# Image copies and Square of layer 2's norm at steps 8 and 12 of the run loop instead of step 15

## The chip, the cores and the metric

The kernel runs on one core of one Trainium2 chip. The core has five engines that work side by side, each through its own queue in order: TensorE (PE, matmuls; PEld is its weight load), VectorE (DVE), ScalarE (ACT), GpSimd (POOL) and SyncE (SP, which here only issues DMAs). Sixteen DMA engines move data between HBM and the on-chip memories. Matmuls write to PSUM. The metric is device time in microseconds (us); less is better.

## The reference, cut to what matters

Four layers follow each other on an image of shape (2, 64, 96, 96): attention over all pixels, a Mamba layer over the pixels in one sequence, a Mamba layer over rows and columns in both directions, and a 3 x 3 filter made from the image's mean. The change is in the third, which the kernel calls layer 2. Its core, with x as (b, c, t, f):

```python
def _rmsnorm(x, w):
    return x * rsqrt(mean(x * x, axis=-1) + EPS) * w

def _mamba(u, p):
    x, z = split(u @ in_proj_w.T)
    x = silu(causal_conv4(x) + conv_b)
    dt, B, C = split(x @ x_proj_w.T)
    dt = softplus(dt @ dt_proj_w.T + dt_proj_b)
    # for each of 128 channels and 16 states, along the sequence:
    h = exp(dt * A) * h + dt * B * x
    y = sum over states of h * C
    return ((y + x * Dp) * silu(z)) @ out_proj_w.T

def _bimamba(u, pf, pb):      # forward, and backward on the flipped sequence
    yf = _mamba(_rmsnorm(u), pf) + u
    yb = flip(_mamba(_rmsnorm(flip(u)), pb) + flip(u))
    return concat(yf, yb)

xt = sequences along t;  xt = xt + _bimamba(xt, P[0], P[1]) @ tlin_w + tlin_b
xf = sequences along f;  xf = xf + _bimamba(xf, P[2], P[3]) @ flin_w + flin_b
```

The norm weight is folded into the projection in the kernel, and both directions share one normalised input.

## The kernel before, in words

**Units.** Layers 1 and 2 are one stream of 120 units, run by `Mamba.run`. A unit is 768 positions (`CH`) of one direction of one batch. Layer 1 gives 24 units. Layer 2 gives 96: first 48 along t, in 24 pairs of a forward and a backward unit over the same eight sequences, then 48 along f. The image is kept on the chip in `k.xb`. Along t a unit reads it with a stride of 96 elements, along f without. The two units of a pair share one `norm`, which belongs to the first (`norm.unit is u`).

**Steps.** A unit has 128 channels x 16 states, that is 16 scans (`STEPS`) of 128 partitions x 768. The loop `for n in range(begin, ...)` in `run` does one step of one unit in each turn:

- `read` (SP, five steps ahead): two DMAs fetch the rows that the step needs from `rows` in HBM into `spread`, one of six buffers.
- `decay` (ScalarE, three steps ahead, L853): two exponentials into h, one of nine buffers.
- `inputs` (VectorE, L863, two steps at a time): `place` in PSUM is `spread` times B.
- `scan` (VectorE, L878), and right behind it on POOL h times C (L879).
- `shared` (TensorE, L857): B for half a unit, into the one PSUM tile for it, issued at step 6 for the second half and at step 14 for the next unit's first half.
- `gather` (TensorE, L888, two steps later): sums h over the states into y.

**Pieces.** All else that a unit needs is cut into pieces, and the table `PIECES` gives each an offset in steps from the unit's own step 0. A piece with offset -49 runs 49 turns before, at step -49 mod 16 = 15 of an earlier unit. Within a turn, `decay` comes first, then `inputs`, `scan` and `gather`, then the pieces of that step whose names are in `reads`, then the others, in the order of the table. The order of instructions on each engine is the order in which this loop issues them; it is written by hand (`manual_schedule`), with no planner. The pieces that matter here, all on one pair's clock (E: the first unit of a pair, O: the second; the norm of a pair is made two pairs ahead, while another pair's units are being scanned):

| piece | engine, line | step |
|---|---|---|
| `gate_read` | ScalarE L772 | 9 of each unit |
| `tail_0`, `tail_1` (the pair before's result) | TensorE L671 | E9, E10 |
| `y_half`, `silu` | ScalarE L892, L775 with two table loads | 10 |
| `tail_read` | ScalarE L924 | E11 |
| `step_mm`, `step_read` | TensorE L671, ScalarE L792, L793 | 11, 13 |
| `step_exp` | ScalarE L797 to L799 | 14 |
| `step_kept` | POOL L806, waits for L799 | 15 |
| `norm_square` | ScalarE L714 twice, L715 | E15 |
| `step_log` | ScalarE L803 | 15 |
| `c_mm`, `c_read` | TensorE, ScalarE L832 | 15, 1 of the next unit |
| `norm_mean` | TensorE L693, into the PSUM tile that `c_read` frees | O1 |
| `norm_root`, `norm_scale` | ScalarE L723, L724, POOL L737 | O3, O10 |
| `step_sum`, `step_dt`, `step_u` | POOL L809, L812, L816, and a memset L820 | 1, 5, 7 |
| `step_write` | SP L825: two DMAs of the unit's dt and dt x to `rows` | 8 |
| `conv`, `conv_read` | TensorE L761, ScalarE L766 | 5, 7 |

The dt that is written at step 8 is that of the next unit; its first `read` follows at step 11 on the same queue, behind the write and behind the reads for steps 14 and 15 of the running unit.

**Buffers.** The normalised input xn has two buffers, sq one. Pieces that need a PSUM tile for a product share one tile `m`, so each waits until the reader of the one before is done.

Of the kernel before, what the change touches and what calls it, by code (L numbers as in the profile page):

```python
# [20 lines left out]
AF = mybir.ActivationFunctionType  # L21
# [10 lines left out]
D_STATE, DT_RANK, D_CONV = 16, 4, 4  # L32
HALF = 4 * W
CH = 2 * HALF
# [33 lines left out]
def rows_of(b):  # L68
    return slice(b * C, (b + 1) * C)
# [551 lines left out]
class Mamba:  # L621
# [79 lines left out]
            u.p = self.mm([(self.t.centre[rows_of(u.b)], self.halves(u.image))])  # L701

    def norm_square(self, u):
        if u.norm.unit is not u:
            return
        u.norm.x = self.work("xn", D_CONV - 1 + CH)
        u.sq = self.work("sq", bufs=1)
        x = u.norm.x[:, D_CONV - 1 :]
        if u.carry:
            self.nc.scalar.activation(u.sq, u.p, AF.Square)  # L710
            self.nc.scalar.copy(x, u.p)
        else:
            for j in range(2):
                self.nc.scalar.copy(x[rows_of(j)].rearrange("p (n t) -> p n t", n=u.image.shape[1]), u.image)  # L714
            self.nc.scalar.activation(u.sq, x, AF.Square)  # L715

    def norm_mean(self, u):
        if u.norm.unit is u:
# [197 lines left out]
    def tail_read(self, u):  # L916
# [10 lines left out]


    PIECES = (
        (-51, "norm_centre"),  # L930
        (-49, "norm_square"),
        (-47, "norm_mean"),
# [34 lines left out]
    def run(self, units, first, n_first, other):  # L967
# [8 lines left out]
        table = [[] for _ in range(self.STEPS)]  # L976
        for offset, name in self.PIECES:
            table[offset % self.STEPS].append((name not in reads, offset, name))
        begin, end = self.PIECES[0][0], self.PIECES[-1][0]


        self.nc.scalar.preload_act_table_set("natural_log_exp_and_others")
        first(0)
        for offset, name in self.PIECES:
            if offset < 0:
# [326 lines left out]
```

## Time and profile before

| | us |
|---|---|
| three runs | 7981.94, 7980.62, 7986.1 |
| median | 7981.94 |
| profiled span | 7974.9 |

The profile is of one execution. Its page gives the busy time of each engine, the chain of work that ended last, and the costliest groups of instructions as: line, engine, operation, what is written <- what is read, shapes, count, then busy us and mean ns of one, then the idle time of the engine just before these instructions and what ended it. "L879 POOL" is line 879 of the kernel on POOL. A list of waits has: engine and line that waited, what it waited for, us in total, times, longest us. A timeline has: start, duration, engine, line, what it does, and in brackets the idle time before and what ended it; neighbours of one kind are merged (x2, x4).

Layer 0 takes the first 2.65 ms or so, layer 1 goes on to about 3.82 ms, layer 2 to 7.89 ms. In layer 2, between 3390 and 7900 us, VectorE is busy 4308 us of 4510, POOL 4063, TensorE 3807 and ScalarE 3405, and the DMA engines are busy for 87 to 90%.

### The profile page before, as it was taken

How to read it: one execution, taken by the hardware profiler on the slowest of the kernel's cores; microseconds unless marked ns; L12 is line 12 of the kernel's file. 1: busy time of each engine (PE TensorE's matmuls, PEld its weight loads, DVE VectorE, ACT ScalarE, POOL GpSimd, SP SyncE). 2: the span in 40 equal slices, each digit the busy share in tenths (PEclk: the TensorE clock that was granted, in tenths of full speed). 3: DMA queues.
4: the chain of work that ended last, by engine and by line, in shares of the span. 5: the costliest groups of instructions: out<-in, count | busy, mean ns of one | idle time of the engine just before them, and what ended most of it. 6: DMA issues, size and time to landing. Idle time of an engine off the chain costs nothing.

```text
span 7974.9 us, 82275 instructions
## 1 busy us (share of the span) xinstructions
PE 7063.0 (89%) x24578; PEld 3122.4 (39%) x24578; DVE 6749.1 (85%) x5524; ACT 5214.3 (65%) x6953; POOL 4724.4 (59%) x3146
## 2 busy tenths in 40 slices
PE   9999999999999788888888888888888888888887
PEld 3333333333333344444444444444444444444443
DVE  6666666666666599999999999999999999999999
ACT  4444444444444577777777777777777777777773
POOL 0000000000000399999888889989889999999985
PEclk9999999999999899999999999999999999999999
DMA  1000000000000388888888888988998899898985
GB/s 43 1 1 1 1 1 1 3 5 5 5 5 3 144 303 317 312 304 325 312 332 325 328 329 329 342 334 328 334 337 334 340 341 347 336 336 335 343 335 205
DMA packets 593806, 1726.06 MB, mean 216 GB/s; under 512 B 65988, under 2 KB 67140, under 8 KB 592840
## 3 DMA queue, kind: packets, MB, share of 16 engines
q1 hardware_dynamic: 591904, 1717.68, 57.9%
q8 instruction: 196, 3.21, 0.2%
q10 hardware_dynamic: 1448, 3.05, 0.1%
q14 instruction: 258, 2.11, 0.1%
HBM read 1522.68 MB, written 197.79 MB: 216 GB/s over the span
## 4 chain that ended last, share of the span: by engine, by line
PE 11%; DMA 10%; ACT 9%; issue 8%; POOL 8%; DVE 4%; SPq 1%; DVEq 0%; ACTq 0%; POOLq 0%
DMA spread<-rows 7%; PE y L888 6%; POOL h L879 6%; ACT h L853 3%; DMA rows<-dtu 3%; PE mm L671 2%; DVE place L863 2%; DVE h L878 1%; PE conv L761 1%; POOL dtu L812 1%; POOL dtu L816 1%; PE y L885 1%; DVE xa L1211 1%; ACT xn L714 1%; PE mm L693 1%
## 5 line engine op out<-in xcount | busy, mean ns | idle before, releaser
L879 POOL TENSOR_TENSOR h<-h,C 128x768 f32<-128x768 f32 x1920 | 3452.4, 1817 | 347.4 <-DVE h L878 310.3
L888 PE MATMUL y<-h,pair 128*128 128x384 f32 x7680 | 2809.6, 510 | 103.4 <-POOL h L879 102.7
L878 DVE TENSOR_TENSOR_SCAN h<-h,place 128x768 f32<-128x768 f32 x1536 | 2606.3, 1737 | 13.6 <-ACT h L853 13.0
L888 PEld LDWEIGHTS y<-h,pair 128*128 128x128 f32 x7680 | 1513.6, 200 | 1306.8 <-POOL h L879 239.6
L311 ACT ACTIVATE e<-f_exp 128x1536 f32<-128x1536 f32 x864 | 1206.4, 1448 | 1224.4 <-PE f_exp L301 1224.4
L853 ACT ACTIVATE h<-spread,xa 128x384 f32<-128x384 f32 x3072 | 1734.3, 608 | 367.0 <-DMA spread<-rows 343.6
L367 DVE TENSOR_TENSOR acc_e<-acc_e,e 128x1536 f32<-128x1536 f32 x792 | 1389.9, 1755 | 683.7 <-ACT e L311 644.8
L863 DVE TENSOR_TENSOR place<-spread,B 128x768 f32<-128x768 f32 x1920 | 1735.0, 948 | 261.9 <-PE B L857 250.8
L340 POOL TENSOR_TENSOR xa<-xa,t_att 64x512 f32<-64x512 f32 x36 | 45.3, 1259 | 2612.3 <-ACT t_att L338 2612.3
L318 PE MATMUL y_att<-e,xb 128*64 128x512 f32 x5184 | 1243.7, 601 | 0.0
L301 PE MATMUL f_exp<-theta,phi 64*128 64x512 f32 x5184 | 1234.6, 607 | 1.0 <-DVE xb L284 0.5
L301 PEld LDWEIGHTS f_exp<-theta,phi 64*128 64x128 f32 x5184 | 466.4, 186 | 754.5 <-issue 460.6
L874 DVE TENSOR_TENSOR_SCAN h<-h,state,place 128x384 f32<-128x384 f32 x768 | 714.0, 990 | 0.0
L318 PEld LDWEIGHTS y_att<-e,xb 128*64 128x64 f32 x5184 | 341.6, 136 | 830.5 <-issue 829.2
L853 ACT ACTIVATE h<-spread,rates 128x384 f32<-128x384 f32 x768 | 433.0, 608 | 150.3 <-DMA spread<-rows 137.5
L885 PE MATMUL y<-raw,xa 128*128 128x384 f32 x384 | 220.4, 663 | 210.5 <-ACT yg L895 182.8
L671 PE MATMUL mm<-raw,xa 128*128 128x384 f32 x768 | 301.2, 517 | 99.2 <-ACT xb L924 91.5
L766 ACT ACTIVATE raw<-conv,cols 128x768 f32<-128x768 f32 x120 | 108.2, 902 | 305.2 <-PE conv L761 240.9
L806 POOL TENSOR_TENSOR kept<-dtu,kept 128x768 f32<-128x768 f32 x120 | 218.3, 1819 | 118.4 <-ACT kept L799 117.9
L761 PE MATMUL conv<-xn,xa 64*128 64x384 f32 (+3 forms) x1536 | 273.1, 494 | 11.7 <-DVE xa L1093 4.0
L892 ACT COPY yg<-y 128x384 f32<-128x384 f32 x120 | 57.4, 478 | 289.7 <-PE mm L671 205.1
L857 PE MATMUL B<-raw,xa 128*128 128x384 f32 x384 | 170.7, 526 | 83.8 <-DVE place L863 83.7
(206 smaller groups left out, 5434.3 us busy)
## 6 DMA issues: line engine op xcount, KB each, us to landing
spread<-rows SPq DMA_DIRECT2D x3840, 384.0 KB, 6.4
rows<-dtu SPq DMA_DIRECT2D x240, 768.0 KB, 5.9
image<-pre SPq DMA_DIRECT2D x11, 384.0 KB, 2.3
xb<-image SPq DMA_DIRECT2D x11, 384.0 KB, 5.8
xa<-in_x SPq DMA_DIRECT2D x1, 2304.0 KB, 23.1
out<-xa ACTq DMA_DIRECT2D x7, 240.0 KB, 2.0
out<-xa SPq DMA_DIRECT2D x1, 1200.0 KB
xa<-in_x SPq DMA_DIRECT2D x3, 384.0 KB, 11.6
```

The lines of the kernel that those rows point to most:

```text
L301: nc.tensor.matmul(fs[j // 3][:, bass.ts(j % 3, NB)], lhsT=phi[at, bass.ts(m // 2, P)], rhs=theta[at, bass.ts(i, NB)], start=True, stop=True,)
L311: nc.scalar.activation(e, f, AF.Exp)
L318: nc.tensor.matmul(y[rows_of(m % 2)], lhsT=g[:, m, :], rhs=es[j // 3][:, bass.ts(j % 3, NB)], start=m < 2, stop=m >= KEYS - 2,)
L367: nc.vector.tensor_add(acc, acc, e)
L671: self.nc.tensor.matmul(o, lhsT=lhsT, rhs=x, start=n == 0, stop=n == len(terms) - 1)
L761: self.nc.tensor.matmul(p3[:, :, o], lhsT=lhsT, rhs=x3[:, :, i], **flags)
L853: self.nc.scalar.activation(h[:, bass.ts(q, HALF)], dt, AF.Exp, scale=u.w.rates[:, n : n + 1])
L863: self.nc.vector.tensor_mul(bx, x, self.B.unsqueeze(1).to_broadcast([P, 2, HALF]))
L874: nc.vector.tensor_tensor_scan(h[:, at], h[:, at], bx[:, at], state[:, q : q + 1], ALU.mult, ALU.add)
L878: nc.vector.tensor_tensor_scan(h[:, way], h[:, way], bx[:, way], 0.0, ALU.mult, ALU.add)
L879: nc.gpsimd.tensor_mul(h2, h2, u.C[:, bass.ts(half, HALF)].unsqueeze(1).to_broadcast([P, 2, HALF]))
L888: self.nc.tensor.matmul(self.y, lhsT=self.t.gather[n], rhs=rhs, start=False, stop=stop)
```

## The change

The piece `norm_square` keeps only what layer 1's units need (`u.carry` is set for these). For layer 2, what it did at E15 in one go is split in two new pieces: `image_0` copies the image to the first 64 partitions of xn at step 8 of E (offset -56), `image_1` copies it to the other 64 and takes the Square at step 12 of E (offset -52). Neither name is in `reads`, so both stand among the last pieces of their step. The convolution and all other pieces stay at their steps. `begin` is the first offset of the table and goes from -51 to -56; the added turns issue nothing.

```diff
     def norm_square(self, u):
-        if u.norm.unit is not u:
-            return
-        u.norm.x = self.work("xn", D_CONV - 1 + CH)
-        u.sq = self.work("sq", bufs=1)
-        x = u.norm.x[:, D_CONV - 1 :]
         if u.carry:
+            u.norm.x = self.work("xn", D_CONV - 1 + CH)
+            u.sq = self.work("sq", bufs=1)
             self.nc.scalar.activation(u.sq, u.p, AF.Square)
-            self.nc.scalar.copy(x, u.p)
-        else:
-            for j in range(2):
-                self.nc.scalar.copy(x[rows_of(j)].rearrange("p (n t) -> p n t", n=u.image.shape[1]), u.image)
-            self.nc.scalar.activation(u.sq, x, AF.Square)
+            self.nc.scalar.copy(u.norm.x[:, D_CONV - 1 :], u.p)
+    def image_copy(self, u, j):
+        if u.norm.unit is u and not u.carry:
+            x = u.norm.x[rows_of(j), D_CONV - 1 :].rearrange("p (n t) -> p n t", n=u.image.shape[1])
+            self.nc.scalar.copy(x, u.image)
+    def image_0(self, u):
+        if u.norm.unit is u and not u.carry:
+            u.norm.x = self.work("xn", D_CONV - 1 + CH)
+        self.image_copy(u, 0)
+    def image_1(self, u):
+        self.image_copy(u, 1)
+        if u.norm.unit is u and not u.carry:
+            u.sq = self.work("sq", bufs=1)
+            self.nc.scalar.activation(u.sq, u.norm.x[:, D_CONV - 1 :], AF.Square)
     PIECES = (
+        (-56, "image_0"),
+        (-52, "image_1"),
         (-51, "norm_centre"),
         (-49, "norm_square"),
```

## The prediction

> **What bounds the kernel now.** I read the page first, then the waits of layer 2, then the timeline of one pair of units. Names: layer 2's 96 units run in 48 pairs; E is the first unit of a pair (the one for which `norm.unit is u`), O the second; E8 is step 8 of E in the run loop, which adds one unit's scan step per turn. The t pairs (0 to 23) read their image with a stride, the f pairs (24 to 47) do not.
>
> The page's first block and two of its groups:
>
> ```profile
> PE 7063.0 (89%) x24578; PEld 3122.4 (39%) x24578; DVE 6749.1 (85%) x5524; ACT 5214.3 (65%) x6953; POOL 4724.4 (59%) x3146
> ...
> L879 POOL TENSOR_TENSOR h<-h,C 128x768 f32<-128x768 f32 x1920 | 3452.4, 1817 | 347.4 <-DVE h L878 310.3
> ...
> L863 DVE TENSOR_TENSOR place<-spread,B 128x768 f32<-128x768 f32 x1920 | 1735.0, 948 | 261.9 <-PE B L857 250.8
> ```
>
> Layer 2 (3823 to 7893 us) is all that the change touches. There VectorE is busy 95% of the time. The scans' start times give 42.4 and 43.5 us for E and O of a t pair and 41.9 and 41.8 in f, against 40.1 us for a unit whose 16 steps run without a stall. So 5.6 us (t) and 3.5 us (f) of a pair are stalls, some 220 us in all. Where they end, over 3900 to 7750 us, by the waits:
>
> ```profile
> ACT h L853 <- DMA spread<-rows: 303.6, 683, 4.1
> POOL h L879 <- DVE h L878: 279.6, 223, 3.8
> ...
> PE mm L693 <- ACT C L832: 157.8, 45, 5.5
> ...
> DVE place L863 <- PE B L857: 134.5, 82, 3.2
> ...
> POOL kept L806 <- ACT kept L799: 77.5, 57, 2.9
> ```
>
> Each L693 wait is `norm_mean` on TensorE at O1, held 3.5 us by ScalarE's `c_read`, 45 times, once a pair. How that comes about, on ScalarE (pair 18; start, duration, in brackets the idle time before):
>
> ```profile
> 5402.72 0.48 ACT L892 COPY yg<-y 128x384 f32<-128x384 f32 x1 [4.03 <-PE mm L671]
> ...
> 5412.38 0.62 ACT L853 ACTIVATE h<-spread,xa 128x384 f32<-128x384 f32 x1 [0.30 <-DMA spread<-rows]
> 5413.02 0.90 ACT L792 ACTIVATE dtu<-mm,cols 128x768 f32<-128x768 f32 x1
> ...
> 5417.36 0.94 ACT L799 ACTIVATE kept<-kept,minus 128x768 f32<-128x768 f32 x1
> ...
> 5419.33 3.13 ACT L714 COPY xn<-xb 64x768 f32<-64x768 f32 x2
> 5422.49 0.84 ACT L715 ACTIVATE sq<-xn 128x768 f32<-128x768 f32 x1
> ...
> 5426.00 0.78 ACT L832 COPY C<-mm 128x768 f32<-128x768 f32 x1
> ```
>
> The reader should see one unbroken block of ScalarE work from 5402.7 (E10) to past `c_read`, with the piece that is moved (L714, L715) near its end, and 4.03 us of idle time ahead of it. Behind `c_read` TensorE has no gap until B for O8 (L857), which comes late, and VectorE stalls: 3.0 us a pair in O0 to O7 (t), 1.6 (f). Pairs 46 and 47, which host no norm, have none there; nor have five of the f pairs, where something else sets the pace.
>
> There is a second circle, and it decides. POOL and ScalarE of the same pair:
>
> ```profile
> 5418.37 1.82 POOL L806 TENSOR_TENSOR kept<-dtu,kept 128x768 f32<-128x768 f32 x1 [1.51 <-ACT kept L799]
> ...
> 5442.05 0.11 POOL L820 MEMSET dtu<- 128x8 f32 x1
> ```
>
> POOL's kept starts 0.08 us after ScalarE's L799 in every E. From there to the memset POOL is all but gapless, 23.3 us. Then SP issues `step_write`, with the `spread` reads queued behind it; from the memset to the next L799 it takes 18.0 us at least (mean 18.3) through DMA, decays and `step_exp`, and so to the next kept. 23.3 + 18.0 + 0.1 = 41.4 us for half a pair, 82.7 for both: f pairs take 83.8.
>
> **What the Trainium skill says.** "PSUM — Partial Sum Buffer", Engine vs sequencer instructions: ScalarE's and GpSimdE's queues are strict FIFO. The trace agrees: L853, L792 and L799 never pass each other. So what stands ahead of `step_exp` delays it. "ScalarE: Activation LUTs", What ACT_TABLE_LOAD costs: about 186 ns plus 0.833 ns an element; for 768 that is 826, and L714 shows 827 ns (f). "SBUF — State Buffer", Door 1: crossing a 16-byte line costs extra; L714 in t, with a stride of 96 elements, shows 1544 ns. "DMA: Bandwidth & Descriptors", Specifications: about 358 GB/s of HBM for a core; the page shows 325 to 347 in layer 2, so a late DMA queue catches up slowly.
>
> **The change, part by part.** No instruction is added or removed, and none is a DMA. Per pair, ScalarE's two copies and Square leave E15: 2 x 1.57 + 0.8 = 3.93 us start to start in t, 2 x 0.84 + 0.8 = 2.48 in f. Of the 48 norms two are hosted in layer 1, 22 (copies of t form) by pairs 0 to 21, 24 (f form) by pairs 22 to 45.
>
> (1) `image_0`, 1.57 or 0.84 us at the end of E8: between its place and L892 ScalarE idles 4.7 us (t), 4.0 (f). `gate_read` (L772) at E9 moves by 0.34 us on average, at most 0.92, and TensorE's tail, which needs its PSUM tile, starts 1.7 us or more after it. Cost nothing: the wait of L892 for TensorE's tail hides it.
>
> (2) `image_1` at the end of E12 (2.36 us t, 1.64 f): it stands ahead of the decays of O0 and O1, `step_read` and `step_exp`. Idle time between its place and L799, for DMA, is 0.34 us (t), 0.60 (f). So L799 and POOL's kept come 1.98 us later in t, 0.99 in f (pair by pair). `c_mm`, which needs `step_read`, has 2.3 us in hand. The decays lose 2 us of 3.6 to 4.9 us ahead of their scans. xn has two buffers and sq one; inside layer 2 their last readers are 17 steps and more back, so there is no new wait. At the layer border the first pair takes its xn buffer two steps ahead of POOL's last copy out of it (L736, 184 ns); that is once in the run and I price it at nothing.
>
> (3) `c_read` then comes earlier by 3.93 - 1.98 = 1.95 us (t), 2.48 - 0.99 = 1.49 (f), `norm_mean` and B with it. Counting for each pair no more than its stall, 43 us (22 pairs) and 28 us (24 pairs): 71 us if VectorE alone counted.
>
> (4) The later kept: the gaps of POOL to the memset take up 0.8 us (t), 0.14 (f), so `step_write` of O is 1.2 and 0.85 us late. Behind it in SP's queue stand the reads for O14, O15 and the next E0; O15's data land 10.2 us or more after the memset. Its slack before its scan is 2.2 us (t), 1.2 (f). So VectorE at O15 gains 1.0 and 0.4 us: 23 + 9 = 31 us instead of 71.
>
> (5) Round the circle: the next kept (O15) waits for L799 too. It had 0.84 us (t), 0.22 us (f) in hand. And TensorE's tail came 0.87 (t), 0.68 us (f) after the least that POOL allows (22.84 us after kept), of which about half is usable. Sum per pair: t 1.98 - 0.8 - 0.84 - 0.4 = -0.06; f 0.99 - 0.14 - 0.22 - 0.5 = +0.13. Carried from pair to pair with each pair's own slacks, -1 us after the t norms and +2 us at the end. The scans' relief is real but lands in a wait for the POOL circle.
>
> The two in layer 1 have wider steps there (2.9 us of VectorE instead of 2.5): nothing. So 7974.9 + 2 = 7977 for the profiled span; the three timed runs have a median 7 us above the span, 7982, so 7984.
>
> **Rivals.** *The scan path decides alone* (faster): VectorE's stall at B is the largest wait of the busiest engine, and it goes. For the whole 71 us, 7911; capped by O15's data, 31 us, 7951. Against it: VectorE idles 4% of an f pair whose circle (82.7 of 83.8 us) has 1% to spare. *`image_1` lengthens the circle* (slower): kept of E waits for ScalarE in every pair, so what `image_1` puts ahead of it passes to `step_write` and the reads behind it. It decides once kept's lateness exceeds the POOL gaps and what O15's kept has in hand: 1.64 us in t, 0.36 in f. If TensorE's tail then gives nothing: 22 x 0.34 + 24 x 0.63 = 23 us, 8005; if the DMA gaps don't take up any of `image_1` either, 22 x 0.38 + 24 x 0.65 = 24 us more, 8029. I carry 8010. *The change does nothing measurable* because all is hidden in DMA waits is the forecast's own neighbour, 7982.
>
> **How the numbers follow.** 0.2%, 16 us, is about what a measurement can tell from no change. Forecast, 7966 to 7998: 0.38. Faster, 7911 to 7965: 0.32. Slower, 7999 to 8035: 0.30. I take the likeliest, 7984. The outer tenth of either rival is left out, which with unknown waits gives 7925 to 8030; the forecast's own range is 7966 to 7998.
>
> **What would show it.** In the changed profile: L714 split, its first copy inside the idle time before L892 (under 3.2 us left); L693's wait for L832 near 2 us instead of 3.5; VectorE's wait for B at O7 mostly gone; and in its place longer waits of POOL's kept for L799 (from 77 us to some 150) and of L863 or L853 for `spread`. If those do not grow, the fast rival is right; if kept's wait grows and B's stall stays, the slow one. What would make me wrong: `image_0` delaying the tail after all, or DMA landings not tied to the memset.

## The result and the profile after

| | before, us | after, us |
|---|---|---|
| median (4 runs each) | 7981.28 | 8025.43 |
| lowest to highest | 7969.58 to 7986.1 | 8019.7 to 8034.75 |
| profiled span | 7974.9 | 8025.4 |

The kernel before has one run more here (7969.58) than in the table ahead of the prediction. The ratio is 1.0059, with a 95% interval of 1.0041 to 1.0076: the changed kernel is slower by 0.6%, 44 us. The forecast was 7984, the range 7925 to 8030; the slower rival was carried at 8010, with a chance of 0.30. So 8025 lies inside the range by 5 us, outside the forecast's own 7966 to 7998, and in the slower rival's band.

The code after image_1 has moved down: what was L799 is L811, L806 is L818, L820 is L832, L853 is L865, L857 is L869, L863 is L875, L888 is L900. The copies are L716, the Square is L727.

First the page of the changed kernel, the costliest groups that answer to those of before (busy us, mean ns, then the idle time before and what ended it):

```profile
PE 7097.7 (88%) x24578; PEld 3127.5 (39%) x24578; DVE 6759.0 (84%) x5524; ACT 5211.1 (65%) x6953; POOL 4720.9 (59%) x3146
...
L891 POOL TENSOR_TENSOR h<-h,C 128x768 f32<-128x768 f32 x1920 | 3449.5, 1816 | 251.8 <-DVE h L890 214.8
...
L875 DVE TENSOR_TENSOR place<-spread,B 128x768 f32<-128x768 f32 x1920 | 1741.1, 950 | 319.6 <-PE B L869 199.6
```

The busy times are the same to within 0.5%, so most of the time is in waits; TensorE's is the one that grew, by 35 us. POOL waits less for VectorE's scans (214.8 us instead of 310.3): VectorE no longer leads. VectorE's wait for B fell only from 250.8 to 199.6 us, and its idle time before L875 grew from 261.9 to 319.6.

The waits of layer 2 in the changed kernel (3900 to 7800 us; total, times, longest):

```profile
ACT h L865 <- DMA spread<-rows: 375.2, 705, 4.0
...
PE y L897 <- ACT yg L907: 246.2, 84, 6.1
...
POOL kept L818 <- ACT kept L811: 188.9, 75, 4.9
DVE place L875 <- PE B L869: 144.1, 116, 3.5
...
PE mm L693 <- ACT C L844: 101.1, 45, 3.1
...
DVE place L875 <- DMA spread<-rows: 45.8, 67, 2.2
```

Two lines of before that the prediction didn't show (3900 to 7750 us):

```profile
PE y L885 <- ACT yg L895: 169.1, 70, 5.2
...
DVE place L863 <- DMA spread<-rows: 8.6, 15, 1.1
```

Four of these waits the prediction had named. `norm_mean` (L693) waits 2.2 us a pair instead of 3.5. POOL's kept waits 189 us for ScalarE instead of 77. For `spread`, VectorE waits 46 us instead of 9 and ScalarE's decays 375 instead of 304. VectorE's wait for B did not fall (144 us, 134 before). One it had not named: TensorE waits 246 us for `y_read` (L907) instead of 169. `y_read` is the piece at step 2 of the next unit with which ScalarE copies the second half of y out of PSUM; TensorE can't start on the next y before that.

ScalarE in pair 18, which starts some 25 us later than before:

```profile
5418.77 1.54 ACT L716 COPY xn<-xb 64x768 f32<-64x768 f32 x1
...
5427.44 0.48 ACT L904 COPY yg<-y 128x384 f32<-128x384 f32 x1 [4.29 <-PE mm L671]
...
5435.92 1.56 ACT L716 COPY xn<-xb 64x768 f32<-64x768 f32 x1
5437.51 0.84 ACT L727 ACTIVATE sq<-xn 128x768 f32<-128x768 f32 x1
5438.26 1.10 ACT L865 ACTIVATE h<-spread,xa 128x384 f32<-128x384 f32 x2
...
5443.73 0.94 ACT L811 ACTIVATE kept<-kept,minus 128x768 f32<-128x768 f32 x1
...
5448.34 0.78 ACT L844 COPY C<-mm 128x768 f32<-128x768 f32 x1
```

From `y_half` (L904) to the start of L811 it takes 16.29 us; before it took 14.64 (5402.72 to 5417.36). From L811 to `c_read` it takes 4.61 us instead of 8.64. That is what the move does to this queue in this pair: 1.65 us more up to L811, 4.03 us less behind it.

And one wait happened only once, at the border of the layers:

```profile
ACT xn L716 <- POOL xn L748: 13.1, 1, 13.1
```

```profile
3684.44 1.52 ACT L716 COPY xn<-xb 64x768 f32<-64x768 f32 x1 [13.07 <-POOL xn L748]
```

The first `image_0` of layer 2 takes an xn buffer out of which POOL still has to make its last copy. ScalarE stands for 13.07 us, and that unit of layer 1 lasts 53.4 us from scan to scan instead of 44.7.

The 50.5 us between the two profiled spans: 3.4 us come before layer 1's first scan, where the two kernels issue the same, 11.5 in layer 1 (8.7 of them in the unit just named), 34.0 in layer 2, 1.6 after it. The busy times that stand ahead of the prediction for layer 2 (3390 to 7900 us) take in the end of layer 1; from 3900 to 7800 us VectorE is busy 3726 of 3900 us before, 3701 after.

### The profile page after: what moved, and what is told of

Same layout as the page of the kernel before. It is cut to its first block, busy times and chain, and to the rows that moved or that the text cites. A ratio compares the mean times of both kernels' runs of the same rounds, so it can differ in the third digit from the quotient of the medians.

```text
span 8025.4 us, 82230 instructions
## 1 busy us (share of the span) xinstructions
PE 7097.7 (88%) x24578; PEld 3127.5 (39%) x24578; DVE 6759.0 (84%) x5524; ACT 5211.1 (65%) x6953; POOL 4720.9 (59%) x3146
## 4 chain that ended last, share of the span: by engine, by line
PE 14%; DMA 10%; POOL 9%; ACT 9%; issue 6%; DVE 3%; SPq 1%; ACTq 0%; DVEq 0%; POOLq 0%
PE y L900 8%; DMA spread<-rows 8%; POOL h L891 6%; ACT h L865 4%; DMA rows<-dtu 3%; PE mm L671 2%; PE conv L773 2%; POOL dtu L828 1%; DVE place L875 1%; PE y L897 1%; POOL dtu L824 1%; PE B L869 1%; DVE xa L1225 1%; ACT L787 1%; ACT raw L787 1%
## 5 line engine op out<-in xcount | busy, mean ns | idle before, releaser
L891 POOL TENSOR_TENSOR h<-h,C 128x768 f32<-128x768 f32 x1920 | 3449.5, 1816 | 251.8 <-DVE h L890 214.8
L900 PE MATMUL y<-h,pair 128*128 128x384 f32 x7680 | 2843.4, 514 | 119.9 <-POOL h L891 117.9
L900 PEld LDWEIGHTS y<-h,pair 128*128 128x128 f32 x7680 | 1519.3, 202 | 1355.9 <-POOL h L891 310.4
L865 ACT ACTIVATE h<-spread,xa 128x384 f32<-128x384 f32 x3072 | 1739.0, 607 | 437.1 <-DMA spread<-rows 411.7
L875 DVE TENSOR_TENSOR place<-spread,B 128x768 f32<-128x768 f32 x1920 | 1741.1, 950 | 319.6 <-PE B L869 199.6
L865 ACT ACTIVATE h<-spread,rates 128x384 f32<-128x384 f32 x768 | 433.8, 608 | 148.6 <-DMA spread<-rows 121.5
L818 POOL TENSOR_TENSOR kept<-dtu,kept 128x768 f32<-128x768 f32 x120 | 218.1, 1817 | 267.1 <-ACT kept L811 240.0
L904 ACT COPY yg<-y 128x384 f32<-128x384 f32 x120 | 57.3, 478 | 295.3 <-PE mm L671 198.3
L869 PE MATMUL B<-raw,xa 128*128 128x384 f32 x384 | 172.2, 530 | 74.1 <-DVE place L875 74.1
## 6 DMA issues: line engine op xcount, KB each, us to landing
xa<-in_x SPq DMA_DIRECT2D x3, 384.0 KB, 11.5
```

What stands on the lines that cost most here:

```text
L865: self.nc.scalar.activation(h[:, bass.ts(q, HALF)], dt, AF.Exp, scale=u.w.rates[:, n : n + 1])
L875: self.nc.vector.tensor_mul(bx, x, self.B.unsqueeze(1).to_broadcast([P, 2, HALF]))
L891: nc.gpsimd.tensor_mul(h2, h2, u.C[:, bass.ts(half, HALF)].unsqueeze(1).to_broadcast([P, 2, HALF]))
L900: self.nc.tensor.matmul(self.y, lhsT=self.t.gather[n], rhs=rhs, start=False, stop=stop)
```

## The experiments

All ratios are to runs of the kernel before on the same chip. All variants of the changed kernel have the border taken out first, since it is a part of its own; their code after the copies stands another 11 lines down in the traces shown (L818 is L829, L907 is L918).

**1. The border alone.** The first pair of layer 2 makes its copies at E15 as before, and does nothing at E8 and E12:

```diff
+            u.border = bool(one.carry) and not u.carry   # first unit of layer 2
     def norm_square(self, u):
...
+        elif u.border:
+            self.image_all(u)          # image_0 and image_1 at E15
```

> The changed kernel, except that the first pair of layer 2 makes its copies and Square at E15 as before, so that image_0 no longer takes the xn buffer ahead of POOL's last copy out of it. In the changed kernel's trace ScalarE waits 13.07 us there, once, and VectorE's unit lasts 53.4 us instead of 44.7. Theory (the border wait is a part of its own, about 9 us): 8025 - 9 = 8016, and no wait of L716 for POOL. If the border is made up for later, 8025; if the border were most of the loss, 7985.

Measured 8014.56 us, ratio 1.0042 (1.0028 to 1.0055), 34 us over the kernel before, where the changed kernel was 44 over it: the border is worth about 10 us (10.3 in the profiles' layer 1), and the rest, 34 us, belongs to the 46 norms inside layer 2. The wait of the first copy for POOL is gone from the trace.

**2. The first copy alone.** `image_1` goes back to E15:

```diff
-        (-52, "image_1"),
...
+        elif u.norm.unit is u:
+            self.image_1(u)            # in norm_square, at E15
```

> image_0 at E8 as in the change, but the second copy and the Square back at E15; border as in the run before. Theory (the circle kept - step_write - L799 sets the pace, image_1 ahead of step_exp lengthens it): L799 keeps its place, c_read comes 1.57 us (t) or 0.84 us (f) earlier, of which the circle lets through what O15's kept had in hand, 0.88 and 0.30 us: 22 x 0.88 + 24 x 0.30 = 27 us faster than before, 7955. If image_0 delays TensorE's tail and that is what costs: slower than before, 8000 or more. If the scan path decided alone: 35 + 20 = 55 us, 7926.

Measured 7949.32 us, ratio 0.9964 (0.9950 to 0.9977): 31 us faster than before. `image_0` in the idle time is not the culprit; it is the good half of the change. From `y_half` to L799's place it takes 14.7 us (t), as before (14.9).

**3. Twice the suspect.** Both copies at E12:

```diff
-        (-56, "image_0"),
+        (-52, "image_0"),
         (-52, "image_1"),
```

> Both copies and the Square at E12, none at E8: 1.57 us (t) or 0.84 us (f) more ahead of step_exp, nothing in the idle time before y_half; border as in the first run of this call. Theory (what stands ahead of step_exp lengthens the circle one for one): 22 x 1.57 + 24 x 0.84 = 55 us slower than the changed kernel without its border wait, 8016 + 55 = 8071. If image_0 at E8 is the culprit: faster than the changed kernel, about 7985. If DMA waits hide what is added: 8016.

Measured 8072.23 us, ratio 1.0117 (1.0101 to 1.0132). One more copy ahead of `step_exp`, 1.57 or 0.84 us, costs 58 us in all, against 55 if it counts one for one. By the scans a t pair grew by 1.66 us and an f pair by 0.60: in t nothing takes it up any more.

**4. All of it in the idle time.** `image_1` behind `gate_read` at E9:

```diff
         (-56, "image_0"),
-        (-52, "image_1"),
+        (-55, "image_1"),
```

> image_0 at E8 and image_1 at E9 behind gate_read, so all of it in ScalarE's idle time before y_half (4.7 us t, 4.0 f, for 3.93 and 2.48 us); border as in the first run of this call. Theory: L799 keeps its place, c_read comes 3.9 or 2.5 us earlier and B's stall at O7 goes; the circle still lets through only 0.88 and 0.30 us a pair: 7955, about as the run with the first copy alone. If the scan path decides once image_1 is out of step_exp's way: 67 + 38 = 105 us, 7876. If ScalarE's later y_half delays everything behind it: 8000 or more.

Measured 7941.86 us, ratio 0.9954 (0.9941 to 0.9968). The waits of this kernel:

```profile
POOL kept L829 <- ACT kept L822: 125.1, 78, 3.3
...
DVE place L886 <- PE B L880: 100.8, 76, 3.5
...
PE mm L693 <- ACT C L855: 30.7, 37, 2.8
```

`norm_mean` waits 0.7 us a pair instead of 3.5, and at O7 VectorE's stalls for B are all but gone (0.5 us over all pairs, 73 before). Yet the gain is 38 us and not the 105 that the stalls from O0 to O7 came to: the scan path doesn't decide alone. What is left of B's stalls is in E, at E7 and E15.

**5 and 6. The circle cut.** POOL's subtraction and addition for the correction of the logarithm are left out, so that nothing on POOL waits for L799; the output lacks the correction:

```diff
     def step_kept(self, u):
-        self.nc.gpsimd.tensor_sub(u.kept, u.e, u.kept)
+        pass
     def step_sum(self, u):
-        self.nc.gpsimd.tensor_add(u.log, u.log, u.kept)
+        pass
```

> The kernel before with POOL's L806 and L809 left out (the correction of the logarithm; the output lacks it), so that POOL waits no more for ScalarE's L799 and has 3.6 us less work in each unit. This cuts the circle kept - step_write - L799. Theory: in the kernel before the circle and the scan path are about equally long, so little is gained, 10 to 50 us: 7930 to 7970. If POOL itself set the pace: 7800 or less.

> The changed kernel without its border wait, and with POOL's L806 and L809 left out as in the run before (the output lacks the correction of the logarithm). Theory: with the circle cut, image_1 ahead of step_exp costs nothing and the earlier c_read counts: 40 to 70 us faster than the run before of this call, where with the circle the change (without the border) was 34 us slower. If what costs is image_1's place in ScalarE's queue, whatever POOL does: some 35 us slower than the run before.

Measured 7926.97 us for the kernel before so cut (ratio 0.9935, 0.9920 to 0.9951), 51 us faster where 10 to 50 were expected, and 7885.00 us for the changed one (0.9889, 0.9874 to 0.9904). The same change, without its border, costs 34 us with the circle and gains 42 us without it. So it is not `image_1`'s place in ScalarE's queue as such that costs; it is that POOL's kept, and what follows it, hangs on that queue. The edit also takes 3.6 us of POOL's work out of each unit, in both kernels. So it makes the circle shorter as well as cutting it, and the two aren't told apart.

**7. The term that was mis-sized: TensorE's tail.** In the kernel of run 1, `y_read` one step earlier:

```diff
-        (18, "y_read"),
+        (17, "y_read"),                # listed ahead of c_read
         (-15, "c_read"),
```

> The changed kernel without its border wait, and y_read one step earlier and ahead of c_read (E1 and O1 instead of 2), so about 1.7 us earlier on ScalarE, c_read 0.46 us later. Theory: TensorE's tail comes 24.2 (t) and 23.9 us (f) after kept, not 22.84, because in E TensorE waits for y_read, which follows L799 of O14; with y_read earlier the tail falls to about 22.9 and L799 of E14 with it: 22 x 1.2 + 24 x 1.0 = 50 us faster than 8015, so 7965. If POOL or TensorE's own work holds the tail: 8015.

Measured 7985.44 us, ratio 1.0008 (0.9999 to 1.0016): 29 us faster than run 1, which it was to beat by 50. One premise was off. `y_read` is not in `reads`, so it came behind `c_read` still, only past one pair of decays:

```profile
5391.73 0.77 ACT L855 COPY C<-mm 128x768 f32<-128x768 f32 x1
5392.41 0.47 ACT L918 COPY yg<-y 128x384 f32<-128x384 f32 x1
5392.78 2.86 ACT L876 ACTIVATE h<-spread,xa 128x384 f32<-128x384 f32 x5
```

So it was 1.1 us earlier, not 1.7. TensorE's tail in E came 23.5 (t) and 23.0 us (f) after kept instead of 24.3 and 23.9, and the whole half from kept to kept fell by 0.64 and 0.56 us. TensorE's tail does hang on `y_read`. VectorE's stalls moved on to the next wait:

```profile
DVE place L886 <- DMA spread<-rows: 97.0, 107, 2.2
...
DVE place L886 <- PE B L880: 72.1, 66, 2.7
```

In run 1 these were 52.1 and 139.9 us.

**8. Copies at E8 and E9, and `y_read` so.** Runs 4 and 7 together.

> The copies at E8 and E9 as in the run that was fastest so far (7942), and y_read one step earlier ahead of c_read. Theory: TensorE's tail in E falls by 1.3 us (t) and 0.9 us (f) here too: 7942 - 29 - 22 = 7891. If in this kernel the DMA part of the circle (41.3 us for half a pair) is all that counts: 46 x 0.5 = 23 us, 7919. If the tail is held by POOL: 7942.

Measured 7921.64 us, ratio 0.9930 (0.9917 to 0.9944). This beats both kernels, and 20 us of it are `y_read`'s. It is the second of the three forecasts, 7919. The tail fell by 0.85 us (t) and 0.76 (f), the half from kept to kept by 0.63 and 0.21 only. From the end of E's memset to L799's end it now takes 18.5 (t) and 18.3 us (f), which is what this link through DMA takes in O: the rest is held there.

**9. `y_read` alone, in the kernel before.** The edit of run 7.

> The kernel before with y_read moved alone: directly behind c_read, ahead of one pair of decays, 1.1 us earlier. Theory: in the kernel before, too, TensorE's tail came 0.9 (t) and 0.7 us (f) after POOL's least in E because of y_read; about half of that goes: 46 x 0.45 = 20 us faster, 7958. If the tail depends on y_read only once O15's kept has nothing in hand, as in the changed kernel: 7970 to 7978, no difference that can be told.

Measured 7965.52 us, ratio 0.9982 (0.9975 to 0.9988): 13 us, between the two forecasts. In f the tail fell from 23.5 to 22.9 us, POOL's least; in t it hardly moved (23.9 to 23.8). Where O15's kept has time in hand, 0.88 us in t, `y_read` isn't what the tail waits for; in f, where it has 0.3, it often is.

**10. `y_read` truly ahead of `c_read`.** As run 8, with the name put in `reads`:

```diff
-        reads = ("y_half", ...
+        reads = ("y_read", "y_half", ...
```

> The copies at E8 and E9, and y_read truly ahead of c_read (in the run of this kind before it came behind it, 1.1 us earlier than at first, not 1.7). Theory: the tail in E falls from 23.6 to about 23.2 us after kept in t and stays at 22.9 in f, and in O c_read comes 0.46 us later, where nothing waits for it now: 22 x 0.3 = 7 us faster than 7922, so 7915. If DMA landings hold the circle by now: 7922.

Measured 7930.99 us, ratio 0.9943 (0.9929 to 0.9956): 9 us slower than run 8, not 7 faster. The tail fell about as forecast (23.6 to 23.4 in t), but the circle did not follow: the half from kept to kept is 42.16 and then 42.07 us in t, 41.64 and 41.76 in f. VectorE's stall for `spread` at E13 grew from 39 to 52 us, which fits a circle held by DMA. The 9 us themselves are not explained: of the 15.3 us between the two profiled spans only 2.9 lie in layer 2, 4.6 in layer 1 and 7.7 before layer 1's first scan.

## Why the prediction was right in its range and wrong in its middle

The range held by 5 us, because it took in most of the slower rival's band; the forecast's own middle, no change, did not come. It was luck in part: 10 of the 44 us are the border, which the prediction had at nothing, and without it the same failed step would have given 8014.

The times between the marks of the circle, from the timelines, means over the norms' 22 t and 24 f pairs, in us. "Tail" is the start of `tail_0` on TensorE, and the memset's time counts from its end:

| | before t | after t | before f | after f |
|---|---|---|---|---|
| kept (O15) to TensorE's tail (E9) | 23.88 | 24.21 | 23.52 | 23.91 |
| `y_half` (E10) to L799's end (E14) | 14.90 | 16.92 | 15.02 | 15.89 |
| kept to kept, E half | 42.44 | 44.78 | 41.81 | 43.08 |
| POOL's gaps from kept (E15) to the memset | 1.18 | 0.31 | 0.20 | 0.06 |
| memset to L799's end (O14) | 18.29 | 18.31 | 18.33 | 18.37 |
| L799's end to kept (O15) | 0.88 | 0.08 | 0.30 | 0.08 |
| kept to kept, O half | 43.65 | 41.93 | 42.08 | 41.74 |

**Step 1, `image_0` costs nothing: right.** ScalarE still waited 4.29 us for TensorE's tail in pair 18, and run 2 gained with it. That less than 3.2 us would be left was wrong: the tail itself comes later, and part of `image_0` went into `gate_read`'s wait for TensorE, which fell from 93 to 61 us.

**Step 2, L799 later by 1.98 and 0.99 us: right,** 2.02 and 0.87 by the table. (The "unbroken block" has short waits for DMA in it, 0.30 us in the lines that it shows; this step counts them.) Its side remark on the border was wrong: what was priced at nothing cost 13.07 us of ScalarE once and about 10 us of time. POOL's copy is short, but it stands behind that unit's scans, two turns of the loop later, and ScalarE's queue stood still until then.

**Step 3, `c_read` earlier: right in size.** It came 1.92 us (t) and 1.64 (f) sooner after `y_half`, and `norm_mean`'s wait fell by 1.44 and 1.13. That VectorE's stall at O7 would mostly go was too much; it went from 73 to 48 us. Why so much of it stayed was not tried.

**Step 4, `step_write` late and VectorE waiting for `spread` at O13 to O15: right.** In O the memset to L799 is the same 18.3 us in every kernel that keeps the correction, and the stalls for `spread` are where they were expected.

**Step 5 failed, in its third term.** POOL's gaps took up 0.87 and 0.14 us (0.8 and 0.14 in the sum), O15's kept gave 0.80 and 0.22 (0.84 and 0.22). The third term was to give 0.4 (t) and 0.5 us (f): that TensorE's tail came 0.87 and 0.68 us after POOL's least was read as slack, "about half" of it usable. (Half of 0.68 is 0.34; with that the forecast for f would have been +0.29.) It gave nothing and took 0.33 and 0.39 instead. So the sum per pair is 2.02 - 0.87 - 0.80 + 0.33 = +0.68 in t and 0.87 - 0.14 - 0.22 + 0.39 = +0.90 in f, where the prediction had -0.06 and +0.13; the scans show 85.9 to 86.5 (without the first pair) and 83.8 to 84.8 us for a pair. Over the pairs, 22 x 0.68 + 24 x 0.90 = 37 us, where the profiles have 34.0 in layer 2. With the border's 10 that is 7981 + 47 = 8028, against 8025 measured.

Why it was no slack shows in TensorE's timeline of pair 18, from E2 to the tail, before and after:

```profile
5381.12 0.91 PE L885 MATMUL y<-raw,xa 128*128 128x384 f32 x2 [2.84 <-ACT yg L895]
5381.87 2.74 PE L888 MATMUL y<-h,pair 128*128 128x384 f32 x8
5385.11 1.56 PE L888 MATMUL y<-h,pair 128*128 128x384 f32 x4 [0.49 <-POOL h L879]
...
5398.98 1.50 PE L671 MATMUL mm<-yg,xa 128*64 128x384 f32 x4
```

```profile
5405.10 1.65 PE L897 MATMUL y<-raw,xa 128*128 128x384 f32 x2 [5.15 <-ACT yg L907]
5406.54 7.44 PE L900 MATMUL y<-h,pair 128*128 128x384 f32 x16
5413.91 2.82 PE L773 MATMUL conv<-xn,xa 64*128 64x384 f32 x16
5416.66 0.91 PE L869 MATMUL B<-raw,xa 128*128 128x384 f32 x2
...
5423.71 1.50 PE L671 MATMUL mm<-yg,xa 128*64 128x384 f32 x4
```

Before, TensorE stood 2.84 us for ScalarE's `y_read` and then now and then for POOL's h. After, it stands 5.15 us for `y_read` and then has no gap for 18.6 us, up to the tail; B for E8 (L869) is in that stretch too, and so E7's stall for B went from 7 to 47 us. `y_read` starts 5.4 us after the end of O14's L799, in t and in f, before and after. So the tail has two parents, POOL's h and ScalarE's L799 one unit earlier, and both lie on the same circle. What O15's kept had in hand helps only along the first; along the second the tail counts from L799. The prediction's pair-by-pair sum had let the tail follow POOL or VectorE, never L799. In f the second was hardly hidden before: there TensorE's gaps in the stretch came to 0.16 us a pair, in t to 1.32 (after: 0.03 and 0.33). Runs 7 and 9 move that parent alone, and the tail follows where POOL doesn't hold it; run 3 shows that by then, in t, nothing takes up what is added.

The second parent is also longer than it need be. Behind the wait 16 matmuls of `gather` (L900) take 7.44 us, where 8 take 2.74 otherwise, and the clock that TensorE was granted (the figure behind the count in brackets; 1.00 is full speed) is 0.68:

```profile
5405.10:5413.91 8.81, 8.81 (x18) 0.68 1.03 401
5413.91:5423.71 9.80, 9.80 (x40) 1.00 0.44 167
```

By the profile's record of that clock, TensorE ran at half speed for part of this stretch in 32 of the 46 pairs before and in 45 after. Its wait for `y_read` there grew from 3.4 to 4.9 us a pair. Over the ten kernels with the correction, TensorE's work in the stretch takes 18.1 us in the 394 pairs with half speed and 16.7 us in the 66 without; it followed all 259 waits of 4 us and more, and 16 of the 46 waits under 2.5 us. An estimate from these figures: with 16.7 us, `y_read` would let the tail start 22.5 us after kept, before POOL's least of 22.84; with 18.1 us, at 23.9, about as measured. So the third term seems to have failed by the clock behind the wait as much as by the wait. No run changes the clock alone, so this part is read from traces and not shown. The nearest to a test is run 4: with `norm_mean`'s wait down to 0.7 us, half speed that began at O2 or O3 in 40 of the 46 pairs before, and in 32 after, was left in 2.

**The rivals.** The slow one was right in its mechanism, and the prediction's own sign pointed to it: kept's wait grew and B's stall stayed. Its first price, "if TensorE's tail then gives nothing", was 8005; the 17 us that the tail took and the border's 10 make 8032 of it, against 8025 measured. Its far price of 8029 is near the measured time by chance, since it let the DMA gaps take up nothing, and they took their part (step 2). The fast one is refuted as a rule for this kernel by run 4; runs 5 and 6 show that the same move does gain, 42 us, once the correction is out.

## What to carry to other kernels

When engines wait for each other in a ring, the busiest engine's stall isn't the price of an edit: find the ring, write down the time of each link, and put moved work where a link waits for something outside its own queue. A link that comes later than its least isn't slack until it is known what else it waits for; look for a second parent before counting on it. A longer wait of TensorE may cost more than its length: look at the clock it was granted behind it. And a buffer that is taken earlier is waited for by the whole queue behind the taker, so check the borders of a loop as well as its middle.

## What the runs showed that was not expected

With `image_1` at E9 the same move gains 38 us (run 4); with it three steps further on, at E12, it loses 34 (run 1), though ScalarE is busy for only 65% of the span. The link from O's memset through DMA to the end of the next L799 kept its 18.2 to 18.4 us in all ten kernels with the correction, while the other links of the pair moved by up to 4 us.
